# Column sums on four 32-column tiles with one float32 matmul, and adapter products by halves of the columns, in a quantised attention and LoRA feed-forward kernel

## The chip, the cores and the metric

The kernel runs on one core of a Trainium2 chip. The metric is the device time of one execution in microseconds. Two kernels are compared by their times on the same chip.

## The reference

Two steps are computed for x of 2 batches x 1024 rows x 2048 columns, in float32:

```python
# step 1: x = x + fake_quant(layernorm(x)) @ fake_quant(ctx)
q = clip(round(v / s + z), 0, 255);  fake_quant(v) = (q - z) * s
# step 2: h = layernorm(x)
x = x + h @ kernel + bias + LoRA(h)
# LoRA(h): per group of 256 rows, rank 32 by the group's gate over 16 adapters,
# plus a shared adapter of rank 32
```

ctx is 2 x 2048 x 2048 and kernel is 2048 x 2048. There are 8 groups, so four for each batch.

## The kernel before

**Step 1.** The two quantised operands are kept as integers around a centre of 128, in bfloat16: c1 (the rows of x) and c2 (the columns of ctx). With zero points z1 and z2, the product of (q1 - z1) and (q2 - z2) is c1 @ c2, plus a term of each row, plus a term of each column, plus a constant. The column term needs the sum of each column of c2 over its 2048 rows. `column_term` (L324 to L329) makes it on TensorE (PE): 16 matmuls of 512 columns (L327, tile pc) with a stationary matrix of ones, so that every one of the 128 partitions of the PSUM tile has the column sums. A VectorE (DVE) instruction, L329, scales pc into a tile of the pool bp. ScalarE (ACT) then fills a PSUM accumulator with this column term and the row term (L340), and 16 matmuls (L342, tile pa) accumulate the product on top. L351 adds the result to the residual y.

The columns are taken in 4 blocks of 512 (n) and the rows in 4 groups of 256 (g), for each of 2 batches, so column_term is called 8 times. `quantise` makes a block of c2 in 8 pieces: ACT (L310) from a loaded tile into one of three buffers q2b, then DVE (L313) into bfloat16. The adapters' gated sums (`gated`, L364, tiles pg_a and pg_b) use matmuls whose outputs are 32 partitions wide, each on a strip of its own of one PSUM bank; L376 copies them into a q2b buffer, L384 transposes pg_a's, and pg_b's go by DMA to a scratch in DRAM (bd).

**Step 2.** The normalised rows are transposed (L413, tile ptz), stored in DRAM (zs) and multiplied by kernel in float32 by a two-level scheme of 7 x 7 products (L590, tiles fu, fv, fw). DVE combines weight tiles and GpSimd (POOL) the rows' tiles (L530, L539), and DVE adds the products to y (L608). The adapters' first product is px (L429). The second is done in small steps among the products by `Delta.step`: ACT fills a two-bank PSUM tile pl with the bias (L459), two matmuls add the product of two groups (L462), each with 64 rows of the array (partitions 0 to 63 and 64 to 127) and each into its own bank, and DVE adds the two banks to y (L472). There are 16 steps in each batch.

**The order.** The program is written in program order. A scheduler decides where each engine's instructions stand among each other, with priorities in a few places (`tc.high_priority`, `tc.issue_after`), and DVE's large additions are tied in a line by `line`. Each engine then runs its own list strictly in order, with waits on the others. The PSUM tiles pc, pg, pt, ptz and px share one pool of two buffers (tag pm). The prefetches of the next batch, its column terms 0 and 1 among them, are made in `meanwhile` during the last of the outer products.

Of the kernel before, what the change touches and what calls it, by code (L numbers as in the profile page):

```python
# [10 lines left out]
F32 = mybir.dt.float32  # L11
# [9 lines left out]
P = 128  # L21
# [45 lines left out]
def tile_quant_xattn_then_lora_ffn(  # L67
# [17 lines left out]
    nc = tc.nc  # L85
    B, S, D = x.shape
    KT = D // P
    MT = S // P
    NB = 512
    NN = D // NB  # L90
    GB, NL = gate.shape
    R = lora_a.shape[0] // NL
# [10 lines left out]
    const = ctx.enter_context(tc.tile_pool(name="const", bufs=1))  # L103
# [4 lines left out]
    ps_m = ctx.enter_context(tc.tile_pool(name="ps_m", bufs=2, space=PSUM))  # L108
# [6 lines left out]
    q2b = Bufs([const.tile([P, 2, NB], I16, tag=f"q2b{i}", name=f"q2b{i}") for i in range(3)])  # L115
# [6 lines left out]
    axT = const.tile([P, GPB // 2, GT], F32, tag="axT", name="axT")  # L122
# [98 lines left out]
    ones_h = const.tile([P, P], BF16, tag="ones_h", name="ones_h")  # L221
    nc.gpsimd.memset(ones_h, 1.0)


    for tag in ("acc0", "acc1", "delta"):
        pi = ps_acc.tile([P, 2, NB], F32, tag=tag, name=f"open_{tag}")
        for i in range(2):
            nc.tensor.matmul(pi[:, i, :], ones_h, ones_h[:, 0:1].to_broadcast([P, NB]), start=True, stop=True)
# [93 lines left out]

    def column_term(b, n, c2):

        pc = ps_m.tile([P, NB], F32, tag="pm", name=f"pc_{b}_{n}")
        for k in range(KT):
            nc.tensor.matmul(pc, ones_h, c2[k // 8][:, k % 8, :], start=(k == 0), stop=(k == KT - 1))  # L327
        colt[n] = bp.take()
        nc.vector.tensor_scalar(colt[n], pc, d1, kdd, ALU.mult, ALU.add)  # L329

# [108 lines left out]
    class Delta:  # L439
# [7 lines left out]
        def step(self):  # L447
            if not self.units:
                return
            pr, n, j = self.units.popleft()  # L450
            cols = ds(n * NB, NB)
            if j == 0:
                self.bp, self.bb = bp.take(), bias_b.take()
                nc.scalar.dma_start(
                    out=self.bp, in_=bd[self.b][ds(2 * pr, 2), :, :, cols].rearrange("g s r n -> (g s r) n")
                )
                nc.scalar.dma_start(out=self.bb, in_=bias[cols].partition_broadcast(P))
            pl = ps_acc.tile([P, 2, NB], F32, tag="delta", name=f"pl_{self.b}_{n}_{pr}_{j}")
            nc.scalar.copy(pl, self.bb.unsqueeze(1).to_broadcast([P, 2, NB]))  # L459
            for i in range(2):  # L460
                rows = slice(i * 2 * R, (i + 1) * 2 * R)
                nc.tensor.matmul(  # L462
                    pl[:, i, :],
                    axT[rows, pr, ds(j * P, P)],
                    self.bp[rows, :],
                    start=False,
                    stop=True,
                    skip_group_check=True,
                )
            for i in range(2):  # L470
                yb = y[2 * pr + i][:, j, cols]
                line(nc.vector.tensor_add(yb, pl[:, i, :], yb))  # L472
            if j == MG - 1:
                bp.give(self.bp)
                bias_b.give(self.bb)


    def line(ins):

        if ins.ins.engine == mybir.EngineType.DVE:  # L480
            if line.last is not None:
                tc.add_manual_dep(
                    ins.ins,
                    line.last.name,
                    mybir.DependencyInfo(mybir.DependencyClass.NoSync, mybir.DependencyReason.DATA),
                    reason="line",
                )
            line.last = ins.ins
# [174 lines left out]
    c2 = {}  # L663
# [8 lines left out]
    for b in range(B):  # L672
# [6 lines left out]
        if b == 0:  # L679
            open_c2(0)  # L680
            prep_x(0, 0, c1T, wk)
            for r in range(NR):
                quantise(c2[0], r)
                if r == 3:
                    prep_x(0, 1, c1T, wk)
            for m in range(4, MT):
                load_x(0, m)
            open_c2(1)
            column_term(b, 0, c2[0])
# [7 lines left out]
        if b == 0:  # L697
            for r in range(4, NR):
                quantise(c2[1], r)
            column_term(b, 1, c2[1])  # L700
        for g in range(2):
            xattn_pair(b, 1, g, c1T, c2[1])
        for g in range(2, GPB):
            for m in range(g * MG, (g + 1) * MG):
                with tc.issue_after(opened.ins):
                    prep_x(b, m, c1T, wk)
            for n in range(2):
                xattn_pair(b, n, g, c1T, c2[n])
                if g + 1 == GPB:
                    close_c2(n)  # L710
                    open_c2(n + 2)
                    bp.give(colt.pop(n))
                    if n == 0:
                        for r in range(NR):
                            quantise(c2[2], r)
                            if r % 4 == 3:
                                lora_a_step(b, r // 4)
                        column_term(b, 2, c2[2])
# [170 lines left out]
```

## Time and profile before

| | |
|---|---|
| median of 3 runs | 1131.94 us (1130.91 to 1132.06) |
| the profiled execution, own time | 1128.31 us |
| its span | 1126.5 us |
| PE busy | 1076.9 us (96%) |
| DVE busy | 734.3 us (65%) |
| ACT, POOL busy | 261.4 us, 263.9 us |
| granted TensorE clock | 1.00 |
| step 1 of batch 0, to the first products of step 2 | about 0 to 192 us |
| step 1 of batch 1 | about 565 to 734 us |

The profile is of one execution. Engines overlap, so busy times do not add up to the span. In the groups, a row has the line, the engine, what is written and read, the shape, the count, the busy time, the mean duration of one, and the idle time before them. The matmuls of a run overlap each other, so their price is the time from one start to the next and not the duration of one. A float32 matmul leaves two records on PE and two weight loads (PEld). Timeline rows begin with the start in us and the length of the merged run.

### The profile page before, as it was taken

What the parts mean: (1) busy time and instruction counts of PE and PEld (TensorE: products, weight loads), DVE (VectorE), ACT (ScalarE), POOL (GpSimd) and SP (SyncE); (2) the same over time, 40 slices, a digit from 0 to 9 for tenths busy, and PEclk for the clock granted to TensorE, in tenths of its full rate; (3) what the DMA queues carried; (4) which work ended last, traced back from release to release, by engine and by line L of the source; (5) the groups of instructions that cost most, each with busy time, mean ns of one, the idle gap of its engine ahead of it and who ended that gap; (6) DMA issues with size and microseconds to landing.
All of it is one profiled execution on the core that took longest, in us unless ns stands there. A gap on an engine that the chain in (4) does not pass through costs nothing.

```text
span 1126.5 us, 10325 instructions
## 1 busy us (share of the span) xinstructions
PE 1076.9 (96%) x3782; PEld 483.3 (43%) x3782; DVE 734.3 (65%) x961; ACT 261.4 (23%) x342; POOL 263.9 (23%) x105
## 2 busy tenths in 40 slices
PE   1689999999999999999999999999999999999998
PEld 0344435544444444444444444455444444444443
DVE  4675538566595767568766654666668586865861
ACT  4975413210001010001384761232000000000000
POOL 0000000234344422525000000022435343243600
PEclk9999999999999999999999999999999999999999
DMA  8991936886689747489866093688668875649611
GB/s 304 395 245 38 294 109 239 306 304 211 247 281 373 265 172 261 158 304 338 302 204 188 1 268 96 235 328 313 233 219 289 298 254 183 253 146 321 213 38 56
DMA packets 120771, 261.33 MB, mean 232 GB/s; under 512 B 11920, under 2 KB 16144, under 8 KB 119568
## 3 DMA queue, kind: packets, MB, share of 16 engines
q1 hardware_dynamic: 99264, 218.65, 57.0%
q10 hardware_dynamic: 21456, 42.02, 10.8%
q8 instruction: 30, 0.49, 0.2%
q14 instruction: 21, 0.17, 0.0%
HBM read 224.99 MB, written 37.75 MB: 233 GB/s over the span
## 4 chain that ended last, share of the span: by engine, by line
PE 81%; DVE 8%; DMA 6%; ACT 4%; issue 1%; SPq 0%; DVEq 0%; ACTq 0%
PE fu L590 33%; PE fv L590 17%; PE pa L342 13%; PE fw L590 8%; PE pl L462 3%; DVE st L279 2%; PE ptz L413 2%; DMA y<-in_x_dram 2%; PE pc L327 2%; DVE big L539 1%; DMA zs<-lit 1%; DMA bd<-q2b 1%; PE pg_a L364 1%; ACT big L291 1%; PE pg_b L364 1%
## 5 line engine op out<-in xcount | busy, mean ns | idle before, releaser
L590 PE MATMUL fu<-big,lit 128*128 128x512 f32 x896 | 396.3, 594 | 0.6 <-DVE y L608 0.6
L539 POOL TENSOR_TENSOR lit<-lit,lit 128x1024 f32<-128x1024 f32 x56 | 161.9, 2898 | 539.5 <-DMA zs<-lit 207.6
L590 PEld LDWEIGHTS fu<-big,lit 128*128 128x128 f32 x896 | 167.7, 190 | 212.4 <-issue 211.4
L342 PE MATMUL pa<-big,big 128*128 128x512 bf16 x1024 | 234.1, 379 | 8.4 <-ACT pa L340 7.2
L590 PE MATMUL fv<-big,lit 128*128 128x512 f32 x448 | 198.1, 594 | 0.0
L530 POOL TENSOR_TENSOR lit<-lit,lit 128x1024 f32<-128x1024 f32 x40 | 101.6, 2539 | 285.6 <-DMA lit<-zs 253.5
L539 DVE TENSOR_TENSOR big<-big,big 128x2048 f32<-128x2048 f32 x56 | 158.9, 2840 | 5.9 <-PE ptz L413 5.3
L608 DVE TENSOR_TENSOR y<-y,fu 128x1024 f32<-128x1024 f32 (+1 forms) x98 | 113.5, 1193 | 69.5 <-PE fu L590 69.2
L342 PEld LDWEIGHTS <-big 128*128 128x128 bf16 x1024 | 97.5, 98 | 139.1 <-issue 31.9
L590 PEld LDWEIGHTS fv<-big,lit 128*128 128x128 f32 x448 | 84.3, 190 | 108.4 <-issue 108.4
L608 DVE TENSOR_TENSOR y<-y,fv 128x1024 f32<-128x1024 f32 x48 | 56.8, 1218 | 92.5 <-PE fv L590 92.5
L459 ACT COPY pl<-bias 128x1024 f32<-128x1024 f32 x32 | 32.6, 1018 | 346.4 <-DVE y L472 320.9
L310 ACT ACTIVATE q2b<-lit,sc,inv 128x1024 int16<-128x1024 f32 x64 | 76.5, 1230 | 139.6 <-DMA lit<-in_ctx_dram 128.1
L530 DVE TENSOR_TENSOR big<-big,big 128x2048 f32<-128x2048 f32 x40 | 100.7, 2517 | 5.1 <-DMA big<-in_w_dram 5.1
L590 PE MATMUL fw<-big,lit 128*128 128x512 f32 x224 | 100.6, 596 | 0.0
L351 DVE SCALAR_TENSOR_TENSOR y<-pa,k_s,y 128x1024 f32<-128x1024 f32 x32 | 41.0, 1282 | 85.6 <-PE pa L342 85.5
L340 ACT ACTIVATE pa<-bp,r_s 128x512 f32<-128x512 f32 x64 | 42.9, 683 | 98.4 <-DVE y L351 35.4
L590 PEld LDWEIGHTS fw<-big,lit 128*128 128x128 f32 x224 | 41.3, 190 | 52.0 <-issue 50.5
L608 DVE TENSOR_TENSOR y<-y,fw 128x1024 f32<-128x1024 f32 x24 | 28.4, 1215 | 52.7 <-PE fw L590 52.7
L299 PE MATMUL pt<-ident_h,big 128*128 128x128 bf16 x256 | 20.5, 231 | 29.9 <-ACT big L294 29.7
L279 DVE BATCH_NORM_STATS2 st<-y 128x6 f32<-128x512 f32 x64 | 41.7, 675 | 2.7 <-DMA y<-in_x_dram 2.7
L472 DVE TENSOR_TENSOR y<-pl,y 128x512 f32<-128x512 f32 x64 | 41.0, 681 | 1.2
(75 smaller groups left out, 591.2 us busy)
## 6 DMA issues: line engine op xcount, KB each, us to landing
big<-in_w_dram SPq DMA_DIRECT2D x96, 1024.0 KB
lit<-zs SPq DMA_DIRECT2D x88, 512.0 KB
lit<-in_ctx_dram SPq DMA_DIRECT2D x64, 512.0 KB
out_dram<-y ACTq DMA_DIRECT2D x30, 512.0 KB
zs<-lit ACTq DMA_DIRECT2D x24, 512.0 KB
y<-in_x_dram SPq DMA_DIRECT2D x8, 1024.0 KB
lit<-in_lora_a_dram SPq DMA_DIRECT2D x32, 256.0 KB
lit<-in_lora_bt_dram SPq DMA_DIRECT2D x32, 256.0 KB
```

Source lines behind the costliest of these rows:

```text
L279: nc.vector.bn_stats(st1[:, m, n, :], ym[:, ds(n * NB, NB)])
L310: nc.scalar.activation(qi, t, AF.Relu, bias=z2, scale=inv2)
L340: nc.scalar.activation(pa[:, j, :], colt[n], AF.Identity, bias=r_s[:, m : m + 1])
L342: nc.tensor.matmul(pa[:, j, :], c1T[g][:, k, ds(j * P, P)], c2[k // 8][:, k % 8, :], start=False, stop=(k == KT - 1), skip_group_check=True,)
L351: summed = nc.vector.scalar_tensor_tensor(yp, pa, s12, yp, ALU.mult, ALU.add)
L459: nc.scalar.copy(pl, self.bb.unsqueeze(1).to_broadcast([P, 2, NB]))
L462: nc.tensor.matmul(pl[:, i, :], axT[rows, pr, ds(j * P, P)], self.bp[rows, :], start=False, stop=True, skip_group_check=True,)
L472: line(nc.vector.tensor_add(yb, pl[:, i, :], yb))
L530: line(eng.tensor_tensor(got[0], got[0], got[1], ALU.add if terms[1][2] > 0 else ALU.subtract))
L539: line(eng.tensor_tensor(out_t, at[p], at[q], op))
L590: nc.tensor.matmul(ps[:, m, :], at[:, k, ds(m * P, P)], bt[:, k, :], start=(opens and k == 0), stop=(ends and k == KQ - 1), skip_group_che ...
L608: line(nc.vector.tensor_tensor(yp, yp, chains[chain][:, js, :], ALU.add if sign > 0 else ALU.subtract))
```

## The change

Two functions are edited.

In `column_term` the 16 matmuls now use only 32 columns of the ones, and matmul k writes to the partitions 32 (k mod 4) to 32 (k mod 4) + 31 of a PSUM tile (pcp). After the 16, each strip of 32 partitions holds the sum over four of the 16 blocks of rows. DVE copies the tile to a q2b buffer as float32, and one float32 matmul with a constant matrix of 1/32 (mean_w, filled once by GpSimd) adds the four strips up and spreads the result over all 128 partitions (pc). The rest is as before.

In `Delta.step` each of the two matmuls is split in two of 256 columns; the order is first half of both groups, then second half of both.

```diff
+    mean_w = const.tile([P, P], F32, tag="mean_w", name="mean_w")
+    nc.gpsimd.memset(mean_w, 1.0 / 32)
...
     def column_term(b, n, c2):
+        parts = ps_m.tile([P, NB], F32, tag="pm", name=f"pcp_{b}_{n}")
+        for k in range(KT):
+            row = P // 4 * (k % 4)
+            nc.tensor.matmul(
+                parts[row : row + P // 4, :],
+                ones_h[:, 0 : P // 4],
+                c2[k // 8][:, k % 8, :],
+                start=(k < 4),
+                stop=(k >= KT - 4),
+                skip_group_check=True,
+            )
+        st = q2b.take()
+        sf = st.rearrange("p k n -> p (k n)").bitcast(F32)
+        nc.vector.tensor_copy(sf, parts)
         pc = ps_m.tile([P, NB], F32, tag="pm", name=f"pc_{b}_{n}")
-        for k in range(KT):
-            nc.tensor.matmul(pc, ones_h, c2[k // 8][:, k % 8, :], start=(k == 0), stop=(k == KT - 1))
+        nc.tensor.matmul(pc, mean_w, sf, start=True, stop=True)
+        q2b.give(st)
         colt[n] = bp.take()
         nc.vector.tensor_scalar(colt[n], pc, d1, kdd, ALU.mult, ALU.add)
...
-            for i in range(2):
-                rows = slice(i * 2 * R, (i + 1) * 2 * R)
-                nc.tensor.matmul(
-                    pl[:, i, :],
-                    axT[rows, pr, ds(j * P, P)],
-                    self.bp[rows, :],
-                    start=False,
-                    stop=True,
-                    skip_group_check=True,
-                )
+            for h in range(2):
+                for i in range(2):
+                    rows = slice(i * 2 * R, (i + 1) * 2 * R)
+                    nc.tensor.matmul(
+                        pl[:, i, ds(h * (NB // 2), NB // 2)],
+                        axT[rows, pr, ds(j * P, P)],
+                        self.bp[rows, ds(h * (NB // 2), NB // 2)],
+                        start=False,
+                        stop=True,
+                        skip_group_check=True,
+                    )
```

In the changed program the scheduler has also placed some neighbouring instructions differently.

## The prediction

> **What bounds the kernel now.** First I read the page's busy times and its 40 slices, to see whether one engine is the limit throughout:
>
> ```profile
> PE 1076.9 (96%) x3782; PEld 483.3 (43%) x3782; DVE 734.3 (65%) x961; ACT 261.4 (23%) x342; POOL 263.9 (23%) x105
> ...
> PE   1689999999999999999999999999999999999998
> ```
>
> TensorE (PE) is 96% busy, and full from the third slice (about 60 us) on. The stretches view gives 30.6 us of PE work in the first 66 us and 1046.3 of 1060 after that. So a microsecond of PE work taken out after 66 us should come off the end; before 66 us PE mostly waits, and a saving there may be swallowed. The granted clock is 1.00 in all stretches.
>
> Next the groups by line, for the two places that are edited and the rows that resemble what replaces them. Columns: count, busy us, mean ns of one. A float32 matmul leaves two records, one for each of its passes.
>
> ```profile
> L327 PE MATMUL pc<-big,ones_h 128*128 128x512 bf16 x128 | 29.6, 384 | 0.0
> L462 PE MATMUL pl<-bp,axT 64*128 64x512 f32 x128 | 36.1, 641 | 2.1 <-ACT pl L459 2.1
> L364 PE MATMUL pg_b<-lit,gmat 128*32 128x512 f32 x64 | 12.7, 605 | 0.0
> ```
>
> pc is 8 column terms of 16 matmuls; pl is 32 steps of two float32 matmuls. Then the timeline, because matmuls overlap and only start-to-start times give their price:
>
> ```profile
> 589.96 3.62 PE L327 MATMUL pc<-big,ones_h 128*128 128x512 bf16 x16
> 593.41 3.83 PE L342 MATMUL pa<-big,big 128*128 128x512 bf16 x17
> ```
>
> A column term costs 593.41 - 589.96 = 3.45 us, 0.216 for each matmul.
>
> ```profile
> 154.76 1.07 PE L364 MATMUL pg_b<-lit,gmat 128*32 128x512 f32 x8
> 155.76 4.49 PE L342 MATMUL pa<-big,big 128*128 128x512 bf16 x20
> 155.97 0.69 DVE L376 COPY q2b<-pg_b 128x512 f32<-128x512 f32 x1 [1.59 <-PE pg_b L364]
> ...
> 171.86 1.05 PE L364 MATMUL pg_b<-lit,gmat 128*32 128x512 f32 x2
> 172.84 3.63 PE L342 MATMUL pa<-big,big 128*128 128x512 bf16 x16
> ```
>
> Four 32-column float32 matmuls (8 records) take 1.00 us, and one alone (2 records) takes 0.98: column tiles run beside each other at the price of one. The stream of one is 0.86 (fu at 210.17, next work at 211.03), so entering and leaving the tiles costs 0.14. The 16 pa matmuls ahead of such a group take 3.56 in the chain instead of 3.45: another 0.11. A trip into tiles and back thus costs 0.25.
>
> ```profile
> 255.00 1.13 PE L462 MATMUL pl<-bp,axT 64*128 64x512 f32 x4
> 256.06 1.12 PE L590 MATMUL fu<-big,lit 128*128 128x512 f32 x2
> ...
> 255.00 0.30 PEld L462 LDWEIGHTS pl<-bp,axT 64*128 64x128 f32 x4 [0.76 <-issue]
> ...
> 234.12 0.38 PE L429 MATMUL px<-lit,acat 128*64 128x256 f32 x1
> 234.13 0.38 PE L429 MATMUL px<-big,acat 128*64 128x256 f32 x1
> 234.34 0.38 PE L429 MATMUL px<-lit,acat 128*64 128x256 f32 x1
> 234.34 0.38 PE L429 MATMUL px<-big,acat 128*64 128x256 f32 x1
> ```
>
> The two row halves of a pl step run together: 1.06 us for what serially would be 4 x 0.43. Its four weight loads (184 ns each) are over in 0.30 us, two by two, the second two while the first pass streams. The px rows show 256-column float32 passes on two tiles: one pair every 0.216 us, each with loads of its own, hidden.
>
> **The change, part by part.**
>
> *Column term, price on PE.* Removed: 3.45 us. Added: 16 matmuls on four 32-column tiles, four at a time, 4 x 0.216 = 0.86, plus the trip 0.25: 1.11. The nearest rows are pg_b's; that 16 short bfloat16 matmuls can be issued so closely is supported by the pt transposes (8 in 0.45 us, 56 ns each, just enough for 16 in 0.9). Then one float32 128x512 matmul: 0.86, up to 0.97 if its first weight load stands open; I take 0.92. Sum 2.03, so 1.42 saved for each of 8 terms, 11.4 in all, if PE never waits and the order stays. Neither holds, so I go through the eight places with the order of the changed program.
>
> *The added wait.* pc must wait for a VectorE copy of the tiles' sums. After a pg_b group the copy begins 0.21 after PE went on and takes 0.69: the result is there 0.95 after the tiles are left. Behind pc in PE's queue stand all the pa matmuls, which ACT, VectorE and the next pairs wait for. The cover is what the program puts between: four pa matmuls (0.86 plus 0.1 of the trip) at term 2, five at term 3, one fu (0.86) at batch 1's term 0. So 0 to 0.1 us each if VectorE is free, as it is there (2.57 us idle ahead of L329 at terms 2 and 3); without that cover 0.9 each, and a 1.28 us L351 in the way would add that.
>
> - Batch 0, term 0 (35.8 us): no cover at all. Copy, float32 matmul and their hand-overs (about 2 us) use up what the tiles save, and ACT is nearly full until 58: 0.
> - Batch 0, term 1 (57 to 66): PE waits 1.68 us for pa's fill after it now; the fill is still behind L351 and L329 on VectorE. About 0.3 of 1.4 is left.
> - Terms 2 of both batches: the copy holds one of the three q2b buffers, so the quantiser's fourth L310 behind it on ACT waits for pc, and the fill of pa_2_0 stands behind that. By the durations (1.23 each, 0.69 for the fill) the fill lands about 0.2 late: 1.2 each.
> - Terms 3: no wait, but the program now sends one pg_b_0 matmul alone and three later, where four went together. By the two pg_b rows one alone costs as much as four: 0.98 + 0.09 lost. 0.35 each.
> - Batch 1, term 0: 1.4.
> - Batch 1, term 1: the tile matmuls are cut into five bursts among pa matmuls: four more trips (1.0) and six groups instead of four (0.43) eat the 1.42: 0.
>
> Sum: 0 + 0.3 + 2 x 1.2 + 2 x 0.35 + 1.4 + 0 = 4.8 us saved. The bounds are 11.4 (no losses) and, with 1.3 us of wait at each of the six places after 66 us, -3.0.
>
> VectorE gets eight copies of 0.69; at 65% busy they hide in its idle time, save for the wait above. The memset of the constant is one GpSimd row of 0.2 us at the start, before anything. SP's queue changes little: two weight loads now go out ahead of eight bd writes after pa_2_3, instead of behind them. They start about 3 us earlier, and the VectorE addition that needs them now stands ahead of y<-pa_3_0. From 2 MB at the 400 GB/s of 164 to 168 us they land about when pa_3_0 ends: 0 to 0.7 late, with 1.9 us of slack before the transposes need it.
>
> *Halves of the columns.* Each step of two matmuls becomes four, with twice the weight loads, the streamed columns unchanged. By the px rows four pair-passes of 0.216 replace two of 0.427: +0.01 a step, +0.3 for 32. The bounds are 0 and, if each of the two added load steps stands open by 0.11 to 0.184 us (the step between the two pairs of loads, and the length of one), 7.0 to 11.8. I take +0.3, because the pl row itself shows the second pair of loads done under the first pass, in the same mode. [...]
>
> *What the stages after it keep.* Between 176 and 242 us (and 715 to 782) ACT waits until 208.8 for a DMA of bp that follows the bd writes, and PE idles 0.8, 0.55, 0.3 and 1.1 us. These writes start from PE's own pg_b_3, so most of the shift carries through; I take 0.3 off. Net: 4.8 - 0.3 - 0.3 = 4.2 us.
>
> **The rivals.**
> 1. *The halves' weight loads stand open.* 32 steps, 7.0 to 11.8 us on a path where PE has no idle time (L590 and L462 follow each other): -4.5 + 7.0 = +2.5, to +7.3: 1134.4 to 1139.2 us. For it: loads and streams would be nearly equal (184 against 216 ns) and no row of before has 256 columns on row tiles. Against it: px, and pl's own overlapped loads. It ends level from 0.14 us a step and is slower by more than 0.2% from 0.21. Chance 0.18.
> 2. *The saving is swallowed.* The waits of the mean matmul come out at a microsecond rather than 0.1 at terms 2, 3 and batch 1's term 0, or the DMA-bound transition does not move with PE: 1.6 us lost in each batch leaves 1.0: 1130.9. Against it: VectorE's idle time at those places. Chance 0.22.
> 3. *The tiles do not run together* because sixteen small loads and matmuls are not issued fast enough: twice the time, +0.86 for 6 terms, 5.2 us: 1132.9, no change. The pg_b and pt rows speak against it; I count it into the second rival's 0.22.
>
> **How the numbers follow.** The profiled execution took 1128.31 us, its span 1126.5, so 1.8 lie around the span; the median of the runs is 1131.94, 3.6 above. I carry the difference over: 1131.94 - 4.2 = 1127.7 (span about 1122.3). The runs of before lie within 1.15 us, so 0.2% (2.26 us) is about what can be told from no change. The forecast (chance 0.60) has its own range of 1125 to 1129.6. The second and third rivals fill 1129.7 to 1134, the first lies above. The range 1124.5 to 1134.5 leaves out most of the first rival and a little below. Chances: faster 0.60, same 0.21, slower 0.19.
>
> **What would show it.** pl's busy time stays near 36 us with twice the records, and fu follows a pl step after 1.06 us; 1.2 or more would be the first rival. pcp's 16 matmuls span about 1.0 us, pc about 0.9 with idle time under 0.2 behind the copy at terms 2 and 3. pg_b should show one group more in each batch, near 1 us each. PE busy falls by about 4 us, with its idle time in the span staying near 50. If PE idle behind the copy exceeds 1 us at several places, or a pl step grows by over 0.14, the forecast is wrong.

## The result, and the profile after

The changed kernel takes **1127.87 us** (median of 5 runs, 1125.5 to 1129.02), the kernel before in the same session 1131.99 us (5 runs, 1130.91 to 1134.04). The ratio is 0.9964, interval 0.9949 to 0.9979: 4.1 us faster, where 4.2 were forecast. In a second session the same pair gave 0.9957 [0.9944, 0.997].

The two first profiles show none of it: 1128.61 us (span 1126.8) for the changed kernel and 1128.31 (1126.5) for the one before. So one pair of profiles could not answer where the gain is, and the kernel before was profiled again (e1 below: 1130.71 us, span 1128.9). The table further down compares stretches of several profiles with that one.

The page of the changed kernel, busy times and PE's row of the 40 slices:

```profile
PE 1072.4 (95%) x3926; PEld 489.3 (43%) x3926; DVE 741.5 (66%) x969; ACT 261.1 (23%) x342; POOL 266.6 (24%) x106
...
PE   1689899999999999999999999999999999999998
```

PE is busy for 4.5 us less, and from the third slice on as full as before, but for the fifth (8 in place of 9). Its groups, for the rows that the prediction named (count, busy us, mean ns, idle time ahead):

```profile
L483 PE MATMUL pl<-bp,axT 64*128 64x256 f32 x256 | 36.3, 402 | 0.4 <-ACT pl L478 0.4
L383 PE MATMUL pg_b<-lit,gmat 128*32 128x512 f32 x64 | 14.8, 605 | 0.0
L333 PE MATMUL pcp<-big,ones_h 128*32 128x512 bf16 x128 | 10.7, 413 | 0.0
L345 PE MATMUL pc<-q2b,mean_w 128*128 128x512 f32 x16 | 9.5, 678 | 0.8 <-DVE q2b L343 0.8
```

The column terms took 29.6 us of PE time; pcp and pc together take 20.2. The groups pg_b cost 2.1 more, about one group more in each batch, as forecast from the split of pg_b_0. The adapters' products pl went from 36.1 to 36.3 with twice the records. The only time that pc waits for the copy is 0.8 us, and the timeline has all of it at 38.33 us, in batch 0's term 0.

PE's idle time in the span did not stay near 50 us: it rose from 49.6 to 54.4. The groups of step 1 and of the transition whose idle time grew (the waits of fu rose by 1.8 us too, and those of pl fell by 1.7):

```profile
L361 PE MATMUL pa<-big,big 128*128 128x512 bf16 x1024 | 238.0, 382 | 11.9 <-ACT pa L359 10.6 <-DVE big L304 1.1
...
L432 PE MATMUL ptz<-ident,big 128*128 128x128 f32 x256 | 35.2, 277 | 2.9 <-ACT axT L456 2.3 <-DVE big L428 0.3 <-ACT lit L433 0.2
```

In the profile of before pa waited 7.2 us for ACT's fills, now 10.6; the transposes of z waited 0.8 for ACT's copy of px, now 2.3. These two waits are followed up in the experiments. pa's busy time is 3.9 us higher: 1.9 us of it lie in its first 16 matmuls, which took 5.53 us where the next 16 took 3.61 (see term 0 of batch 0 below). The rest goes with shorter runs, 89 in place of 77.

A step of the adapters' products in the timeline of the changed kernel:

```profile
256.39 0.73 PEld L483 LDWEIGHTS pl<-bp,axT 64*128 64x128 f32 x8 [0.76 <-issue]
256.40 1.13 PE L483 MATMUL pl<-bp,axT 64*128 64x256 f32 x8
...
257.46 1.12 PE L611 MATMUL fu<-big,lit 128*128 128x512 f32 x2
```

fu follows after 257.46 - 256.40 = 1.06 us, the same as with whole products. The eight weight loads (186 ns each) begin in pairs at 256.39, 256.50, 256.72 and 256.93 and are over in 0.73 us; each pair after the first runs while the passes before it stream. This is against the first rival: the added loads are for the same two row groups as the ones before them, and none of them stands open.

Term 2 of batch 0 in the timeline of the changed kernel:

```profile
113.37 1.47 PE L361 MATMUL pa<-big,big 128*128 128x512 bf16 x6
114.88 0.69 ACT L359 ACTIVATE pa<-bp,r_s 128x512 f32<-128x512 f32 x1 [1.16 <-PE pa L361]
...
115.62 0.38 PE L361 MATMUL pa<-big,big 128*128 128x512 bf16 x1 [0.78 <-ACT pa L359]
116.36 1.05 PE L333 MATMUL pcp<-big,ones_h 128*32 128x512 bf16 x16
117.34 1.04 PE L361 MATMUL pa<-big,big 128*128 128x512 bf16 x4
117.46 0.69 DVE L343 COPY q2b<-pcp 128x512 f32<-128x512 f32 x1
118.21 1.12 PE L345 MATMUL pc<-q2b,mean_w 128*128 128x512 f32 x2
119.17 7.07 PE L361 MATMUL pa<-big,big 128*128 128x512 bf16 x32
```

The tiles take 117.34 - 116.36 = 0.98 us and the mean matmul 119.17 - 118.21 = 0.96. The copy begins 0.12 after PE has gone on, is done at 118.15, and pc starts at 118.21: four pa matmuls hide it. One cost of the new order was not in the prediction: a seventh pa matmul now stands ahead of the transposes that come before the tiles, and it waits 0.78 us for ACT's fill. In the kernel before the transposes themselves waited 0.42 there for the copy of pg_a, so the net cost is 0.36.

Term 0 of batch 1 shows the price between float32 matmuls, in the second profile of the changed kernel (e4 below):

```profile
582.57 1.08 PE L611 MATMUL fu<-big,lit 128*128 128x512 f32 x2
583.58 1.05 PE L333 MATMUL pcp<-big,ones_h 128*32 128x512 bf16 x16
584.55 1.12 PE L611 MATMUL fu<-big,lit 128*128 128x512 f32 x2
585.52 1.03 PE L345 MATMUL pc<-q2b,mean_w 128*128 128x512 f32 x2
586.38 1.02 PE L611 MATMUL fu<-big,lit 128*128 128x512 f32 x2
...
588.17 0.38 PE L361 MATMUL pa<-big,big 128*128 128x512 bf16 x1
```

and in the second profile of the kernel before (e1 below), with the same three fu and 16 transposes around the term:

```profile
583.08 1.08 PE L590 MATMUL fu<-big,lit 128*128 128x512 f32 x2
583.99 3.62 PE L327 MATMUL pc<-big,ones_h 128*128 128x512 bf16 x15
...
590.17 3.40 PE L327 MATMUL pc<-big,ones_h 128*128 128x512 bf16 x15
```

The two pieces take 0.97 + 0.86 = 1.83 us in place of 3.45. Part of the trip is paid by their neighbours: the fu ahead takes 1.01 (0.91 in e1), the one between the tiles and pc 0.97 (0.86 behind pc). With them, the stretch takes 588.17 - 582.57 = 5.60 us in place of 590.17 - 583.08 = 7.09: 1.49 saved, where the prediction's general price saves 1.42.

### The profile page after: what moved, and what is told of

It reads as the page before. It is cut to its first block, busy times and chain, and to the rows that moved or that the text cites. A ratio compares the mean times of both kernels' runs of the same rounds, so it can differ in the third digit from the quotient of the medians.

```text
span 1126.8 us, 10619 instructions
## 1 busy us (share of the span) xinstructions
PE 1072.4 (95%) x3926; PEld 489.3 (43%) x3926; DVE 741.5 (66%) x969; ACT 261.1 (23%) x342; POOL 266.6 (24%) x106
## 4 chain that ended last, share of the span: by engine, by line
PE 80%; DMA 7%; DVE 6%; ACT 4%; issue 1%; SPq 1%; ACTq 0%; DVEq 0%
PE fu L611 33%; PE fv L611 17%; PE pa L361 13%; PE fw L611 9%; DMA lit<-in_ctx_dram 4%; PE pl L483 3%; PE ptz L432 2%; DVE big L560 1%; PE pg_a L383 1%; DVE st L283 1%; PE pg_b L383 1%; ACT big L298 1%; ACT big L295 1%; DMA bd<-q2b 1%; DMA big<-in_w_dram 1%
## 5 line engine op out<-in xcount | busy, mean ns | idle before, releaser
L361 PE MATMUL pa<-big,big 128*128 128x512 bf16 x1024 | 238.0, 382 | 11.9 <-ACT pa L359 10.6
L303 PE MATMUL pt<-ident_h,big 128*128 128x128 bf16 x256 | 20.3, 231 | 29.6 <-ACT big L298 29.4
L317 DVE TENSOR_SCALAR big<-q2b 128x1024 bf16<-128x1024 int16 x64 | 27.6, 440 | 23.7 <-ACT q2b L314 20.5
```

Source lines behind the costliest of these rows:

```text
L317: nc.vector.tensor_scalar(c2[r // 4][:, ds(2 * (r % 4), 2), :], qi, QMAX, CENTRE, ALU.min, ALU.subtract)
L361: nc.tensor.matmul(pa[:, j, :], c1T[g][:, k, ds(j * P, P)], c2[k // 8][:, k % 8, :], start=False, stop=(k == KT - 1), skip_group_check=True,)
```

## The experiments

The prediction's account is theory A: PE work taken out after 66 us comes off the end, less what waits and transitions keep. Its rivals are the open weight loads of the halves (C in some of the texts), a saving that is swallowed, and a saving that is worth the same wherever the term stands (D). For the waits around term 2 a further one (E) came up: they depend on when the loads of ctx land and on ACT's order, not on the q2b buffer that holds the strips' sums. Ratios are to the kernel before on the same chip, in the same session.

**e1, the kernel before again** (no edit).

> The kernel before, unchanged, profiled and timed once more. The profiled execution of before took 1128.31 us, its other executions 1130.9 to 1134.0. Theory A (the gain of 4.1 us lies in PE work that is taken out, as predicted): this trace has its end near 1130 us of span and the same landmarks as the first up to 176 us, and the 3.6 us between the executions lie in one of the two transitions from step 1 to step 2, where ACT waits for a DMA. Rival B (the difference of the medians is mostly a matter of when the DMAs land, and not of the PE work): the two traces of before differ by as much as before and after do. Ratio to before: 1.000 within 0.002.

Measured: 1131.56 us (1130.05 to 1133.74), ratio 0.9992 [0.9981, 1.0002]. Its second transition (from the first transposes of z in batch 1 to the second batch of px) took 54.65 us, that of the first profile of before 52.39. These 2.26 us, and a slower start of the first profile of after, are why those two look level.

**e2, the column term alone.** The adapters' products are whole, as before.

> The new column term alone; the adapters' products stay whole. Theory A: 4.2 us faster than before (ratio 0.996), and the landmarks of the changed kernel's trace: about 2 us later than before by the start of the third column term in batch 0, 1.5 us gained at terms 0 and 1 of batch 1, 1.3 and 0.45 at its terms 2 and 3. Rival B: no clear difference from before (0.999 to 1.001).

Measured: 1129.61 us (1126.13 to 1130.38), ratio 0.9967 [0.9954, 0.998]. The column term alone gives a gain that is clear of noise, and by e3 the halves give none; e2's ratio is nearer to 1 than e4's below, but their intervals overlap. The 1.3 us expected at term 2 of batch 1 did not come in this trace: that stretch is 0.44 longer.

**e3, the halves alone.** column_term is as before.

> The halves of the columns alone; the column term stays as before. Theory A: +0.3 us in the sum, no difference that can be measured (ratio 0.999 to 1.001), a pl step of 1.06 us and PE busy with pl 36.3 us. Rival C (the open weight loads, first rival of the prediction): 7 to 12 us slower, 1.006 to 1.010. If this kernel is 4 us faster, the gain comes from the halves and not from the column term.

Measured: 1133.74 us (1131.21 to 1141.13), ratio 1.0021 [1.0007, 1.0036]. A ratio within 0.001 of 1 was expected. pl is 36.3 us and a step 1.06, as in the whole change. The profiled execution was the fastest of its runs and lies 0.5 us above e1's profile; the 1.8 us of the medians are in no trace. By the prediction's estimate open loads would have cost 7 us or more.

**e4, the change again** (no edit).

> The changed kernel, unchanged, profiled and timed once more, on the chip of the three others. Theory A: ratio 0.996 again, and a trace with the same gains and losses at the eight places as the first one: +1.5 to +2 us at terms 0 and 1 of batch 0, -1.5 at those of batch 1, -1.3 and -0.45 at its terms 2 and 3. Rival B: ratio nearer 1.000 and other landmarks.

Measured: 1127.61 us (1127.24 to 1127.99), ratio 0.9957 [0.9944, 0.997]; profile 1127.24 us. The 1.5 to 2 us of loss that were expected at terms 0 and 1 of batch 0, after the first profile, came out as 0.1.

**e5, only the two early terms of batch 0 in the new form**, with the halves, and **e6, only the other terms but batch 1's term 1**:

```diff
     def column_term(b, n, c2):
+        if not (n < 2 and b == 0):        # e5;  e6: if n < 2 and (b == 0 or n == 1):
+            ...                           # the old form: 16 matmuls with ones_h into pc
+            return
```

> The halves as in the change, but the new column term only for terms 0 and 1 of batch 0, where TensorE waits for others anyway; the other six keep 16 whole matmuls. Theory A (a saving counts only where TensorE is the limit): no gain, the transposes of group 2 start 0 to 0.3 us later than in before, 1.3 us later when the mean matmul meets the half clock; ratio 0.999 to 1.002. Rival D (a term saves its 1.4 us wherever it stands): 2.8 us faster, 0.9975.

> The change, with the old 16 matmuls at the three terms to which the prediction gave nothing or 0.3 us: 0 and 1 of batch 0 and 1 of batch 1. Theory A: as fast as the whole change or up to 1 us faster (ratio 0.995 to 0.9965), with 1.2 to 1.5 us gained at term 0 of batch 1. Rival D: 4.2 us slower than the change, the ratio near 1.000.

Measured: e5 1132.66 us (1131.13 to 1135.97), ratio 1.0007 [0.9997, 1.0017]; e6 1128.08 us (1125.74 to 1131.18), ratio 0.997 [0.996, 0.998]. Two terms before 66 us bring nothing that can be told from noise; the five later ones bring what the whole change does, as far as the intervals can tell (its ratio was 0.9957 in another session). A saving that counts wherever it stands (D) would have shown in e5.

**e7, the strips' sums staged in axT**, which is idle in step 1, so that no q2b buffer is held:

```diff
-        st = q2b.take()
-        sf = st.rearrange("p k n -> p (k n)").bitcast(F32)
+        sf = axT.rearrange("p a t -> p (a t)")
         nc.vector.tensor_copy(sf, parts)
```

> The change, with the tiles' sums staged in the tile axT, which is idle at these times, instead of in one of the quantiser's three q2b buffers. Theory A (the quantiser waits on ACT for the buffer that pc holds, and the accumulators' fills stand behind it): no ACT wait for pc at L314 any more, 0.2 to 1 us gained at each of terms 2, and at terms 0 and 1 of batch 0; 0.5 to 2 us faster than the change, ratio 0.994 to 0.996. Rival E (the fills wait for the loads of ctx or for the order on ACT, not for the buffer): the same as the change, 0.996.

Measured: 1133.6 us (1128.9 to 1137.49), ratio 1.0013 [1.0, 1.0026]; the profiled execution is its fastest run. Neither expectation came out: the gain is gone in the medians. By the stretches the profile is still 2.0 us shorter than e1's, where e4's is 3.5. In the trace the loss shows at term 2 of batch 1: the stretch from 644 to 674 us of the table below is 1.14 us longer than in e1, where e4's is 0.80 shorter. ACT and PE there, in e7:

```profile
665.19 1.24 ACT L314 ACTIVATE q2b<-lit,sc,inv 128x1024 int16<-128x1024 f32 x1 [1.09 <-DMA lit<-in_ctx_dram]
...
667.06 2.32 PE L359 MATMUL pa<-big,big 128*128 128x512 bf16 x10 [2.77 <-ACT pa L357]
```

and the same place in e4, with the q2b buffer held:

```profile
663.46 1.24 ACT L314 ACTIVATE q2b<-lit,sc,inv 128x1024 int16<-128x1024 f32 x1 [0.32 <-DMA lit<-in_ctx_dram]
...
665.33 4.04 PE L361 MATMUL pa<-big,big 128*128 128x512 bf16 x17 [0.51 <-ACT pa L359]
```

PE waits for the fill of pa in both, and the fill stands behind a quantise piece that waits for a load of ctx: 2.77 us in e7, 0.51 in e4. In e2, whose column terms are those of e4, with the buffer held, it is 1.76:

```profile
665.58 1.24 ACT L314 ACTIVATE q2b<-lit,sc,inv 128x1024 int16<-128x1024 f32 x1 [1.57 <-DMA lit<-in_ctx_dram]
...
667.45 5.56 PE L361 MATMUL pa<-big,big 128*128 128x512 bf16 x24 [1.76 <-ACT pa L359]
```

In the first profile of the changed kernel there is no such wait. So the buffer of the strips is not the cause of it; the landing of the loads and ACT's order are (E). Whether the edit itself makes the loads land later is not shown. Why e7's other runs are up to 8.6 us above its profile no trace shows.

**e8, the whole change, with the load of the adapters' sums sent off by GpSimd:**

```diff
-                nc.scalar.dma_start(
+                nc.gpsimd.dma_start(
                     out=self.bp, in_=bd[self.b][...]
```

> The change, with the load of bp from bd issued by GpSimd instead of ACT, so that ACT does not stand behind the landing of the bd writes in the two transitions from step 1 to step 2. Theory A (the transitions give back 0.5 to 0.9 us of the saving each, because ACT stands there until a time that the DMAs set): TensorE idles less there, and the kernel is 0.5 to 2 us faster than the change, ratio 0.994 to 0.996. Rival F (the transition is set by other loads, or GpSimd now stands where ACT stood and delays its additions): same as the change or slower, 0.996 to 0.998.

Measured: 1126.66 us (1124.21 to 1127.79), ratio 0.9952 [0.9939, 0.9964]. The chain that it cuts, in e4:

```profile
748.55 0.33 ACTq L473 DMA_DIRECT2D bp<-bd  x1
748.92 0.37 ACT L456 COPY axT<-px 128x256 f32<-128x256 f32 x1 [10.38 <-DMA bd<-q2b]
...
749.35 0.66 PE L432 MATMUL ptz<-ident,big 128*128 128x128 f32 x4 [1.03 <-ACT axT L456]
```

ACT's copy of px stands behind its issue of bp: it starts at 748.92, 0.37 us after that issue, and after 10.38 us of idle time that the bd writes end. PE then waits 1.03 us for the copy. In e8, where GpSimd sends bp off, the copy is at 744.14, 4.8 us earlier than in e4, after 7.99 us of idle time that px itself ends. Half of the 4.8 was gained ahead of this point, since px too starts 2.4 us earlier in e8. Counted from the start of px, the copy comes after 7.18 us in e8 and after 9.56 in e4.

**e9, the same edit on the kernel before** (its control).

> The kernel before with nothing changed but the engine that sends off the load of the adapters' sums in each batch (bp from bd): GpSimd in place of ACT, as in e8. It is the control for e8. If that load alone blocked ACT in the transitions (the transposed sums axT were copied at 749.65 us in the profile of before, and about 4 us earlier in e8), this kernel gains by itself what e8 gains over e4 in the medians: 1 to 2 us, so about 1130.5 (ratio 0.9985 to 0.999), and its copies into axT stand 3 to 5 us earlier than in e1. If ACT in the transitions is held up only once the column terms are cheaper (the swallowed saving), this kernel stays within 0.5 us of before. With both in full e8's gain is the sum of e4's and this one's.

Measured: 1130.52 us (1129.01 to 1134.15), ratio 0.9983 [0.997, 0.9995]. The copy in batch 1 is 2.05 us earlier than in e1 (749.31 against 751.36), less than the 3 to 5 expected, but counted from the start of px it gains the 2.4 of e8 again (7.17 against 9.57). The two transitions are 1.05 and 1.89 us shorter. So the block on ACT costs the kernel before as well; it is not made by the change. That e8 is faster than e4 by as much is not shown: their ratios, 0.9952 and 0.9957, come from two sessions and can't be told apart.

**e10, e6 with e8's edit**, and **e11, the same with whole products.**

> The change with the old form kept where the new one brought nothing (both early terms of batch 0, and term 1 of batch 1), as in e6, and with the adapters' load sent off by GpSimd, as in e8. If the gain is PE work taken out after 66 us and the two parts are independent, this is the fastest so far: 1125.5 to 1127 (ratio 0.994 to 0.9955), no worse than e8 by over 0.5 us. If what e6 seemed to keep was the spread of its runs, it lies 1 us or more above e8 (1127.7 or more).

> e10 with the adapters' products whole again (two matmuls of 512 columns a step in place of four of 256). It settles the halves' effect beside the same kernel. Open weight loads would make e10 slower than this by 7 us or more, which the traces already speak against; the prediction's term was 0.3 us, so this should lie 0 to 0.5 us below e10. The run of the halves alone (e3) measured 1.8 us slower in the median but 0.5 in the trace: if those 1.8 are a cost of the halves, this kernel is 1.5 to 2 us faster than e10; if the lower medians of e4 beside e2 were the halves' doing, it is 1.5 to 2 us slower.

Measured: e10 1126.99 us (1125.94 to 1132.17), ratio 0.9957 [0.9941, 0.9973]; e11 1126.56 us (1125.72 to 1128.11), ratio 0.9949 [0.9932, 0.9966]. Side by side the halves cost 0.4 us in the medians, which the spread of the runs would hide. e3's 1.8 us do not come back here. The three versions e8, e10 and e11 can't be told apart; each beats the kernel before by about 5 us.

**e12, e10 with term 3 one row group later:**

```diff
-            if g == 2:
+            if g == 3:
                 column_term(b, 3, c2[3])
```

> e10 with column term 3 called one group of rows later (after the last of the four row groups of n = 2 has been sent its products, in place of the third). The first group of the adapters' gated sums is then not split any more, which the prediction priced at 1.07 us for each batch, but the mean matmul has less work of PE ahead of it to cover the copy of the strips, up to 0.9 us for each batch, and the fill of the next block's accumulator stands closer behind it. If the split is the larger term, 0.5 to 2 us faster than e10; if the cover is, level or up to 1.5 us slower, with PE idle ahead of the third mean matmul near 0.9 us.

Measured: 1155.09 us (1151.41 to 1159.48), ratio 1.0199 [1.0175, 1.0223]: 28 us slower than e10, which no theory had. Both small terms of the expectation came out in the trace: pg_b is back at 12.5 us for its 64 records (14.8 in e10), and the mean matmul waits 1.43 us in batch 0, because a VectorE addition of 1.28 us stands ahead of the copy. Together with the split that is gone they cost 0.9 us in each batch against e10, and the stretch of term 2 in batch 1 costs 1.4. Nearly all of the rest arises in the transitions, 14.7 us in the first and 8.4 in the second. VectorE in e12 there:

```profile
201.26 2.29 DVE L557 TENSOR_TENSOR big<-big,big 128x2048 f32<-128x2048 f32 x1 [4.47 <-DMA big<-in_w_dram]
203.47 1.53 DVE L434 TENSOR_SCALAR big<-y,mv_z,rstd_z 128x1024 f32<-128x1024 f32 x2
```

and PE:

```profile
204.42 1.77 PE L438 MATMUL ptz<-ident,big 128*128 128x128 f32 x8 [4.11 <-DVE big L434]
```

At 227.93 us PE waits for such a normalisation again, 7.19 us. The scheduler has put a combination of weight tiles, which waits for its load, ahead of the normalisation that PE's transposes need. In e10 no combination stands between the last normalisations (195.55 to 199.60 us), and PE waits for none of them before px. Of the 25 us between the profiles of e12 and e10, 20 are idle time of PE and 5 are busy time. PE runs slower in e12 for a while: eight transposes and the two records of fu behind them take 1.73 and 1.71 us from start to start at 227.93 us, and 0.88 and 0.86 at 208.93 in e10. In e12 the granted clock is 0.50 from 204.7 to 208, 225.2 to 231.9 and 757.6 to 760.9 us, where e10 has 1.00. Moving a step of 2 us by one group cost more than ten times what the step is worth.

**Where the gain is, stretch by stretch.** Starts of the same records were compared in the traces; the numbers are the length in e1 and the difference to it, in us (minus is shorter). "After" is the first profile of the changed kernel.

| stretch (e1, us) | e1 | after | e4 | e2 column | e3 halves | e6 late |
|---|---|---|---|---|---|---|
| 23 to 50: batch 0, term 0 | 26.61 | +1.92 | +0.55 | +0.57 | +0.09 | +0.85 |
| 50 to 77: term 1 | 27.22 | -0.43 | -0.44 | -0.43 | 0 | 0 |
| 77 to 132: term 2 | 54.84 | +0.62 | -0.54 | -0.32 | +0.02 | -0.85 |
| 132 to 177: term 3 | 45.12 | -0.44 | -0.44 | -0.44 | -0.01 | -0.44 |
| 177 to 231: transition | 54.20 | -0.56 | +0.23 | +0.97 | +0.50 | +0.37 |
| 231 to 572: products | 340.24 | +0.07 | +0.07 | -0.03 | +0.06 | +0.06 |
| 572 to 644: batch 1, terms 0, 1 | 72.67 | -1.55 | -1.55 | -1.54 | -0.01 | -1.96 |
| 644 to 674: term 2 | 29.32 | -1.23 | -0.80 | +0.44 | 0 | -1.23 |
| 674 to 719: term 3 | 45.11 | -0.43 | -0.43 | -0.43 | +0.01 | -0.43 |
| 719 to 773: transition | 54.65 | -0.25 | -0.26 | +0.01 | -0.19 | -0.51 |
| 773 to 1123: products | 349.81 | +0.07 | +0.07 | 0 | +0.08 | +0.07 |

The sums are -2.2 us for after, -3.5 for e4, -1.2 for e2, +0.5 for e3 and -4.1 for e6. One profile each, they scatter more than the medians, by which e4 is 4.4 us and e2 2.4 faster than the kernel before in their session. e6 has the old form in the first two rows and in half of the seventh.

## Why the prediction was right, step by step

The forecast's mechanism and its sign held, and the sum is near. Its terms did not all hold; some of the closeness is errors of both signs, and that part is luck.

- **The price of a term.** 2.03 us forecast; the two pieces take 1.94 at term 2 of batch 0 and 1.83 at term 0 of batch 1. The forecast counted 0.11 of the trip in the run ahead of the tiles, and at the second place the neighbours do pay about that: 1.49 saved against 1.42 forecast. This step held.
- **The added wait.** At terms 2 and 3 pc waits at most 0.1 us, by the cover that was named. e12 shows the other bound: with cover gone and an addition in the way it is 1.43.
- **Batch 0, term 0.** Forecast 0. The new form lies at +0.55 to +1.92 in this stretch, but e6, with the old form there, is at +0.85, so a loss is not shown. What moves this stretch from profile to profile is the pace of PE's matmuls. The prediction read a granted clock of 1.00 in all stretches, and the first profile of after reads 1.00 around 38.33 us too, but the starts of the matmuls show two paces: in the kernel before, matmuls of 512 columns start 0.43 us apart until 36.9 us, and 0.216 apart after it. In e1 this ends at 36.7 us, in e6 at 38.3; about four matmuls at 0.43 in place of 0.216 make e6's +0.85. With the new form PE is slow once more: in e2, e4, e5, e7 and e8 the granted clock reads 0.50 for 3.4 us between 40.1 and 45.6 us, and in the first profile of after the starts are 0.43 apart until 46.2. There the mean matmul took 2.07 us where e4 has 1.13, and 16 pa matmuls from 42.31 us took 5.53 where the next 16 took 3.61. None of the eight profiles with the old form at this term shows such a second slow stretch. What brings it on is not shown. The wait of 0.80 without cover is as forecast.
- **Terms 1 and 3.** Forecast 0.3 and 0.35 each; measured 0.43 and 0.44. The split of pg_b_0 costs about what the two rows said.
- **Terms 2.** Forecast 1.2 each; measured from a loss of 0.62 to a gain of 0.85 in batch 0, and from a loss of 0.44 to a gain of 1.23 in batch 1. This step failed: the held q2b buffer was named as the reason for a wait of 0.2, and e7 and e2 show that the landing of the ctx loads sets it, between nothing and 2.8 us in batch 1.
- **Batch 1, terms 0 and 1.** Forecast 1.4 and 0; measured 1.55 together, of which term 0 gives 1.49 and term 1 in its five bursts next to nothing, as forecast. With term 1 in the old form (e6) the stretch is 1.96 shorter, but that is not a price of the bursts: PE's wait for the copies of the transposes near 617 us is 0.30 there, and 0.62 and 0.51 in e1 and e4.
- **The halves.** Forecast +0.3; the two stretches of products, where nearly all of the 32 steps lie, grow by 0.14 with them and by 0 without (e2). Nothing else of it is shown in a trace.
- **The transitions.** Forecast 0.3 kept in all. They keep 1.0 in one of the traces of the new column term (e2) and give 0.8 back in another (the first of after). bp's issue on ACT follows the bd writes, as the prediction said; that this makes the scatter is not shown, and two profiles of the kernel before differ by 2.26 us in the second transition. That the wait is also a price of the kernel before, and can be had back by another engine (e9), was not in the prediction.
- **The rivals.** The first fell (pl 36.3 us, step 1.06). The tiles do run together: 16 matmuls in 0.98 us. The second holds in part: of about 11 us that eight terms could have saved, waits and splits kept over half, as the forecast's own sum had it.
- **The carried difference** of 3.6 us between the profile and the median of before was luck of one profile: e1's profile lies 0.85 below its median. The forecast stood because it was made against the median.

## What to carry to other kernels

Price a replaced group from start to start at its place, with its neighbours, and count the saving only where PE is full: two cheaper terms before 66 us were worth nothing that can be measured (e5, ratio 1.0007), the later ones all of it (e6, 0.997). Before a copy is put between two matmuls, look for the work that covers it, and for the long instruction on the copying engine that could stand ahead of it: with cover PE waited at most 0.1 us at terms 2 and 3; in e12, with the cover gone and an addition of 1.28 us in the way, 1.43. Where a scheduler fixes the order, moving a step of 2 us lengthened the two transitions by 23 together, so read each engine's order after the edit. Let a transfer that waits for other transfers be sent off by an engine that nobody waits for: in e8 and e9 the copy of px came 2.4 us sooner after px than in e4 and e1.

## What the runs showed that was not expected

- In a step of pl the weight loads for the same row groups ran under float32 matmuls of only 256 columns: eight loads in 0.73 us, and the step stayed at 1.06.
- A trip from float32 matmuls of the full array to four 32-column tiles and back cost about 0.3 us at term 0 of batch 1, spread over three pieces: 1.01 for the float32 matmul ahead (0.91 elsewhere), 0.97 for 16 bfloat16 matmuls on the tiles (4 x 0.216 = 0.86 of streaming), 0.97 for the float32 matmul behind (0.86 elsewhere).
- The bfloat16 matmuls of 512 columns started 0.43 us apart at first and 0.216 apart later; the last slow stretch of this start ended between 36.7 and 46.2 us, by profile, and moved the first stretch of the table by up to 2 us.
- Two profiles of one program differed by 2.26 us in a single transition (52.39 and 54.65), more than half of this change.
